# One of eight encoder blocks: which weight tiles are summed by transfers, by ones and by VectorE

## The chip, the core and the metric

The kernel runs on one core of one Trainium2 chip. The metric is the device time of one execution in microseconds (us), median of several executions. TensorE (PE) multiplies matrices, VectorE (DVE) works on whole tiles elementwise, ScalarE (ACT) computes functions such as tanh and exp, GpSimd (POOL) here mostly issues transfers, and SyncE (SP) only issues transfers. Sixteen DMA engines move the data.

## The reference, cut to what matters

Two graph attention layers stand behind one another, each added to its input; N is 4096 nodes, with four heads of 128 features. The change lies in the encoder, the first attention of the first layer:

```python
h = jnp.maximum(_layernorm(x, axis=-1), 0.0)
Xw = jnp.einsum('hnd,hde->hne', Xh, W)            # per head
f1 = jnp.einsum('hnd,hd->hn', Xw, V[:, 0, :, 0])
f2 = jnp.einsum('hnd,hd->hn', Xw, V[:, 1, :, 0])
sig = jax.nn.sigmoid(f1[:, :, None] + f2[:, None, :])
att = _masked_softmax(adj[None] * sig, adj != 0)   # local and long pattern are both adj
Xa = jnp.einsum('hij,hjd->hid', att, Xw)
Xn = _batchnorm(Xc, enc_bn_gamma, enc_bn_beta)     # Xc: the heads side by side
```

So each output row is a sum over neighbours of weight times value, divided by the sum of the same weights. That second sum, the denominator, is what the change concerns. After the encoder come a matrix product with batch normalization, a decoder that uses the same weights again, another product, and the second layer with an attention of its own.

## The kernel before

**Tiles and blocks.** Weights are made transposed: a tile `e` holds 128 source nodes (partitions) by 2048 target nodes. An attention works through blocks; a block is one head `h` and one half `tb` of the targets, so there are eight, numbered n = 0 to 7. "Block three" below is n = 2, the first half of head two; "block four" is n = 3. In a block, `j` runs over 32 source tiles. The whole encoder is one loop over n and j in `attention` (lines 395 to 516).

**What happens for one j.** A buffer is taken for `e` (line 420). ScalarE computes a tanh into it (line 570) and an exp in place (line 571). VectorE multiplies it with the adjacency tile `a` (line 572). TensorE multiplies it with the head's values in four matrix products, one for each 512 targets, which accumulate over j in four PSUM banks `po` (line 469). The third and fourth step of the same loop make the sum for the denominator, in one of three ways, chosen by j:

- *moved* (line 489): GpSimd issues two accumulating transfers, one for each half of the tile, that add `e` to a second sum tile named `acc` in the profile (`into` in the code). The first moved tile of a block is copied instead, which overwrites the old sum.
- *by ones* (line 267): TensorE multiplies the tile with a 128 by 32 matrix of ones, four narrow products next to each other in the array, into the bank `den`. Neighbouring j of this kind are held back and done together.
- *added* (lines 497 and 499): VectorE adds the tile to `acc`. The first such instruction takes two tiles.

At j = 31 both sum tiles are themselves multiplied with ones into `den` (lines 514 and 516). The next block's first moved tile has to wait for that, because it overwrites the sum tile that this product reads.

**Buffers.** `weight_tile` (line 254) deals out eight buffers in turn: two shared with the decoder and six of the block (`ebufs` is 6, plus `EP` = 2). As 32 is a multiple of eight, tile j always gets the buffer of tile j − 8, and ScalarE's tanh into it waits until everyone who reads tile j − 8 is done: its matrix products, its sum (transfers included), and for every fifth tile (j = 4, 9, 14, ...) a store to memory that the decoder reads later.

**The end of a block, inside the next.** VectorE copies the four banks out in step j = 2 of the next block (line 682), copies `den` at j = 4 (line 273), and inverts the row sums at j = 10 (lines 283 and 284). GpSimd's queue, which is in order, carries the hops of the row sums between its moves: `dens` out and `dcol` in at j = 4, `rinvs` at j = 10, four loads of `rb` from j = 11 on (lines 274, 279, 287, 292). A move behind such a hop waits for it. VectorE scales and takes statistics as these arrive (lines 686 and 689).

**Choice by block.** `modes` (line 401) gives each block its moved and its by-ones tiles:

```python
ENC_FIRST = (), (5, 6, 11, 12, 17, 18, 24, 25, 30, 31)
ENC_SECOND = (12, 14, 17, 19, 22, 24, 26), (1, 2, 4, 5, 7, 8, 30, 31)
ENC = (0, 2, 5, 7, 10, 12, 15, 17, 20, 22, 25), (8, 9, 30, 31)
```

`ENC` holds for n = 2 to 7. The core of the sums:

```python
if j in moved:
    for into_half, e_half in in_parts(2, into, e):
        nc.gpsimd.dma_start(into_half, e_half, **({"accum_op": ALU.add} if j > moved[0] else {}))
elif j in by_ones:
    held.append(e)
```

In block three SyncE also loads the 1 MB of encoder weights (`encoder_weights`, at j = 8).

Of the kernel before, what the change touches and what calls it, by code (L numbers as in the profile page):

```python
# [60 lines left out]

ENC_FIRST = (), (5, 6, 11, 12, 17, 18, 24, 25, 30, 31)
ENC_SECOND = (12, 14, 17, 19, 22, 24, 26), (1, 2, 4, 5, 7, 8, 30, 31)
ENC = (0, 2, 5, 7, 10, 12, 15, 17, 20, 22, 25), (8, 9, 30, 31)

GAT_FIRST = (0, 2, 4, 6, 8, 10, 12, 14, 16, 18, 20, 22, 24), (30, 31)
# [23 lines left out]
def kernel(ctx, tc, x, xT, adjT, w0, w0T, v0, wencT, wdecT, vecs, w1, w1T, a1, outT):  # L90
# [486 lines left out]
    with tc.tile_pool(name="keep", bufs=1) as keep:  # L577

        with tc.tile_pool(name="f_small", bufs=1) as small, tc.tile_pool(name="f_work", bufs=2) as work:
# [5 lines left out]
            for ib in range(NIB):  # L585
# [7 lines left out]
                for c in range(0, C, 1 if ib == 0 else C):  # L593
                    n = 1 if ib == 0 else C
# [125 lines left out]
        with tc.tile_pool(name="enc", bufs=1) as spool:  # L720

            with tc.issue_after(last_copy.ins), tc.issue_after(masks0[-1][1].ins):
                attention("enc", keep, spool, tanh_weights, R[0:4], lambda h, tb: (rows[tb], h), out_enc,
                          (scaled, statistics), 6, lambda n: (ENC_FIRST, ENC_SECOND, ENC)[min(n, 2)],
                          (TINY, ALU.max), "write", row0=row0, masks0=masks0,
                          extras={(2, 8): encoder_weights, (H * NTB - 1, 10): coefs_of_three,
                                  (H * NTB - 1, 12): bias_of_three, (H * NTB - 1, 20): scale_three})
# [399 lines left out]
```

## Time and profile before

| | us |
|---|---|
| median of three executions | 3204.63 (3203.29 to 3204.93) |
| the profiled execution | 3203.78 |
| span from its first to its last instruction | 3202.0 |

| engine | busy us | share of the span |
|---|---|---|
| TensorE | 3144.9 | 98% |
| VectorE | 2937.1 | 92% |
| ScalarE | 2573.6 | 80% |
| GpSimd | 526.1 | 16% |

The mean granted TensorE clock is 0.997. The encoder takes roughly the first 1034 us of the span. Times below are us from the span's start; a block is counted from the end of the last matrix product of the block before it to the end of its own last one: block two ends at 320.4, block three at 438.9, block four at 559.1, then every 118.2 up to 913.7. In the list of groups an entry gives line, engine, operation, tiles, count, total busy time, mean duration and the idle time ahead of it. In a timeline an entry gives start, duration, engine, line, operation, number of merged instructions, and in brackets the idle time ahead of it with what ended it. A start to the next start is a little shorter than the duration, as neighbouring instructions of an engine overlap by about 0.1 us.

### The profile page before, as it was taken

The page shows a single profiled execution, that of the slowest core. Times are in us where ns is not written, and L with a number is a line of the kernel's source. Part 1 is how long each engine was busy: PE and PEld are TensorE (multiplying, and loading weights), DVE is VectorE, ACT ScalarE, POOL GpSimd, SP SyncE. Part 2 cuts the span into 40 slices and gives each one's busy share as a digit, 9 for nine tenths or more (in the row PEclk, how much of TensorE's full clock was granted, in tenths as well). Part 3 has the DMA queues.
Part 4 walks back from the last instruction along what each step waited for, and adds up shares of the span by engine and source line. Part 5 has one row for each costly group of instructions (what it writes and reads, how often), then busy time and mean ns, then how long its engine had stood idle before and what let it go on. Part 6 is the DMA issues. An engine that isn't in the chain of part 4 may idle for free.

```text
span 3202.0 us, 30044 instructions
## 1 busy us (share of the span) xinstructions
PE 3144.9 (98%) x10531; PEld 1369.0 (43%) x10531; DVE 2937.1 (92%) x2221; ACT 2573.6 (80%) x1825; POOL 526.1 (16%) x684
## 2 busy tenths in 40 slices
PE   7999999999999999999999999999999999999998
PEld 6334444444444463333333333458544444444443
DVE  7989999999999679999999999785699999999998
ACT  7999999999998449999999999466755665666663
POOL 3001211211211000010100100026312222222211
PEclk9999999999999999999999999999999999999999
DMA  9999988988987014445445454231579999999996
GB/s 211 198 194 253 269 225 229 268 220 230 273 232 194 7 41 147 158 144 169 156 161 166 144 170 145 91 110 63 155 189 233 215 222 241 218 214 230 236 213 156
DMA packets 215367, 591.33 MB, mean 185 GB/s; under 512 B 25936, under 2 KB 29040, under 8 KB 199216
## 3 DMA queue, kind: packets, MB, share of 16 engines
q0 software_dynamic: 71584, 234.05, 38.3%
q1 hardware_dynamic: 132200, 332.53, 30.2%
q10 hardware_dynamic: 11432, 22.85, 2.0%
q8 instruction: 82, 1.34, 0.2%
q14 instruction: 69, 0.57, 0.1%
HBM read 378.15 MB, written 84.30 MB: 144 GB/s over the span
## 4 chain that ended last, share of the span: by engine, by line
PE 55%; DVE 22%; issue 10%; DMA 9%; ACT 4%; DVEq 0%; POOL 0%; ACTq 0%; SPq 0%; POOLq 0%
PE ps L331 22%; PE ps L469 14%; PE ps L738 7%; DVE e L1044 7%; DVE R L499 6%; DMA w<-e 6%; DVE e L572 4%; PE den L331 3%; PE ps L949 3%; DVE acc L499 3%; DMA a<-mask 3%; ACT e L570 2%; PE den L267 2%; ACT e L571 1%; PE ps L798 1%
## 5 line engine op out<-in xcount | busy, mean ns | idle before, releaser
L469 PE MATMUL ps<-e,R 128*128 128x512 f32 x3992 | 1738.0, 595 | 25.9 <-DVE e L572 21.5
L469 PEld LDWEIGHTS ps<-e,R 128*128 128x128 f32 x3992 | 753.4, 190 | 1006.8 <-issue 919.6
L572 DVE TENSOR_TENSOR e<-e,a 128x2048 f32<-128x2048 f32 (+1 forms) x470 | 1050.0, 2262 | 88.2 <-ACT e L571 75.3
L570 ACT ACTIVATE e<-rowb,score 128x2048 f32<-128x2048 f32 (+1 forms) x470 | 909.5, 1970 | 25.0 <-PE ps L331 9.0
L571 ACT ACTIVATE e<-e 128x2048 f32<-128x2048 f32 (+1 forms) x470 | 866.9, 1880 | 6.4 <-DVE e L572 3.0
L331 PE MATMUL ps<-e,R 128*64 128x512 f32 x2624 | 746.9, 592 | 1.6 <-DVE e L572 1.5
L1043 ACT ACTIVATE e<-rowb,nq,jcol 128x2048 f32<-128x2048 f32 x224 | 459.6, 2088 | 263.2 <-DMA w<-e 133.8
L1044 DVE SCALAR_TENSOR_TENSOR e<-e,jcol,a 128x2048 f32<-128x2048 f32 (+1 forms) x265 | 592.0, 2266 | 2.8 <-ACT e L1043 2.8
L331 PEld LDWEIGHTS ps<-e,R 128*64 128x64 f32 x2624 | 241.8, 137 | 319.8 <-issue 316.2
L499 DVE TENSOR_TENSOR R<-R,e 128x2048 f32<-128x2048 f32 x128 | 291.7, 2279 | 0.0
L499 DVE TENSOR_TENSOR acc<-acc,e 128x2048 f32<-128x2048 f32 x121 | 276.4, 2284 | 0.9
L489 POOL DMA_DIRECT2D w<-e x178 | 149.2, 847 | 610.7 <-DMA w<-e 282.4
L738 PE MATMUL ps<-R,w 128*128 128x512 f32 x512 | 220.4, 592 | 0.6 <-DVE w L696 0.6
L489 POOL DMA_DIRECT2D acc<-e x146 | 122.6, 891 | 520.9 <-DMA acc<-e 212.6
L331 PE MATMUL den<-e,R 128*64 128x512 f32 x320 | 149.8, 592 | 0.0
L738 PEld LDWEIGHTS ps<-R,w 128*128 128x128 f32 x512 | 97.1, 190 | 123.0 <-issue 117.4
L331 PE MATMUL ps<-e,w 128*64 128x512 f32 x288 | 138.1, 592 | 0.7 <-DVE e L572 0.7
L292 POOL DMA_DIRECT2D rb<-rinvs x60 | 33.8, 568 | 521.0 <-DVE R L686 453.3
L949 PE MATMUL ps<-w1x,hT 128*128 128x260 f32 x512 | 115.5, 384 | 1.4 <-ACT hT L927 1.4
L331 PE MATMUL ps<-t,w 128*64 128x512 f32 x336 | 111.2, 592 | 1.0 <-DVE t L340 1.0
L949 PEld LDWEIGHTS ps<-w1x,hT 128*128 128x128 f32 x512 | 96.5, 190 | 19.9 <-issue 3.3
L331 PE MATMUL ps<-t,R 128*64 128x512 f32 x192 | 90.2, 592 | 0.0
(209 smaller groups left out, 2109.9 us busy)
## 6 DMA issues: line engine op xcount, KB each, us to landing
a<-mask SPq DMA_DIRECT2D x720, 256.0 KB, 4.2
w<-e POOLq DMA_DIRECT2D x178, 512.0 KB, 6.7
acc<-e POOLq DMA_DIRECT2D x146, 512.0 KB, 6.9
e<-ekeep SPq DMA_DIRECT2D x48, 1024.0 KB, 5.1
ekeep<-e SPq DMA_DIRECT2D x36, 1024.0 KB, 6.9
mask<-in_adjT POOLq DMA_DIRECT2D x8, 2048.0 KB, 105.3
rowb<-rows SPq DMA_DIRECT2D x16, 1024.0 KB, 6.1
rb<-rinvs POOLq DMA_DIRECT2D x60, 256.0 KB, 4.8
```

Source lines behind the costliest of these rows:

```text
L267: last_ones = nc.tensor.matmul(den[s * 32:(s + 1) * 32, :], ones[:, 0:32], t[:, s * IB:(s + 1) * IB], start=start, stop=stop)
L331: last_half = nc.tensor.matmul(b[g * HD:(g + 1) * HD, :], weight, x, start=start, stop=stop)
L469: last_main = nc.tensor.matmul(b, block(values[h], j), e[:, s * IB:(s + 1) * IB], start=(j == 0), stop=(j == NJ - 1))
L489: nc.gpsimd.dma_start(into_half, e_half, **({"accum_op": ALU.add} if j > moved[0] else {}))
L499: nc.vector.tensor_add(acc, acc, e)
L570: nc.scalar.activation(e, rowb, AF.Tanh, bias=column(score[:, 1], j, h), scale=0.5)
L571: last_act = nc.scalar.activation(e, e, AF.Exp, scale=0.5)
L572: last_dve = nc.vector.tensor_mul(e, e, a)
L738: last = nc.tensor.matmul(z, w[:, fb, o * P:(o + 1) * P], nodes(src[fb], ib), start=(fb == 0), stop=(fb == C - 1))
L949: m = nc.tensor.matmul(banks[k][:, 0:2 * DX], hT[:, fb, c * P:(c + 1) * P], w1x[:, fb, 2 * k:2 * k + 2, :].rearrange("p h x -> p (h x)"), ...
L1043: last_act = nc.scalar.activation(e, rowb, AF.Relu, bias=column(nq, j, h), scale=column(jcol, j, h))
L1044: last_dve = nc.vector.scalar_tensor_tensor(e, e, column(jcol2, j, h), a, ALU.add, ALU.mult)
```

## The change

Block three (n = 2) gets a choice of its own; all other blocks keep theirs.

```diff
 ENC_SECOND = (12, 14, 17, 19, 22, 24, 26), (1, 2, 4, 5, 7, 8, 30, 31)
+ENC_THIRD = (0, 3, 6, 9, 12, 15, 18, 21, 24), (7, 8, 16, 30, 31)
 ENC = (0, 2, 5, 7, 10, 12, 15, 17, 20, 22, 25), (8, 9, 30, 31)
...
-                          (scaled, statistics), 6, lambda n: (ENC_FIRST, ENC_SECOND, ENC)[min(n, 2)],
+                          (scaled, statistics), 6, lambda n: (ENC_FIRST, ENC_SECOND, ENC_THIRD, ENC)[min(n, 3)],
```

In block three nine tiles are moved instead of eleven, each three steps after the last instead of two and three in turn. Five tiles instead of four are summed by ones (7, 8, 16, 30, 31 for 8, 9, 30, 31). The remaining eighteen instead of seventeen are added by VectorE, in seventeen instructions instead of sixteen.

## The prediction

> **What bounds the kernel now.** The page puts TensorE at 98% of the span, but a change to one block must be read in that block. So I first cut the encoder by blocks in the table of windows, then asked who waits for whom in block three, then read the timelines of ScalarE, GpSimd, TensorE and VectorE there. The windows of blocks two to five (length; busy time of PE, PEld, DVE, ACT, POOL; clock; DMA share):
>
> ```profile
> 206.00:320.40 114.40, 111.06 (x295) 46.41 (x297) 108.35 (x60) 111.04 (x60) 15.54 (x21) 1.00 0.95 236
> 320.40:438.90 118.50, 116.59 (x309) 49.52 (x312) 113.32 (x63) 112.42 (x61) 22.37 (x29) 1.00 0.90 247
> 438.90:559.10 120.20, 118.13 (x308) 50.11 (x310) 114.47 (x64) 120.20 (x66) 22.38 (x29) 0.99 0.88 237
> 559.10:677.30 118.20, 116.57 (x309) 49.51 (x312) 114.36 (x64) 118.20 (x65) 22.35 (x29) 1.00 0.90 241
> ```
>
> From block four on ScalarE is busy for the whole window: 120.20 of 120.20, 118.20 of 118.20. One tile costs it 3.693 us (two tanh and two exp start every 7.386 us), so 32 tiles cost 118.2 us, the length of a block. The list of waits of ScalarE between 404 and 1030 us is empty. From block four to the end of the encoder ScalarE sets the pace, and whatever delays it earlier is carried along to the end. Block three is the last in which it waits, 6.1 us (118.50 − 112.42). Who makes it wait there (total, times, longest):
>
> ```profile
> POOL acc L489 <- DMA acc<-e: 36.5, 12, 6.0
> ...
> DVE e L572 <- ACT e L571: 5.0, 5, 2.3
> ACT e L570 <- DMA acc<-e: 4.4, 3, 2.5
> ...
> ACT e L570 <- issue: 0.6, 1, 0.6
> ```
>
> The timeline of ScalarE shows where:
>
> ```profile
> 360.14 2.00 ACT L570 ACTIVATE e<-rowb,score 128x2048 f32<-128x2048 f32 x1 [1.63 <-DMA acc<-e]
> ...
> 390.75 2.00 ACT L570 ACTIVATE e<-rowb,score 128x2048 f32<-128x2048 f32 x1 [0.61 <-issue]
> ...
> 400.78 2.00 ACT L570 ACTIVATE e<-rowb,score 128x2048 f32<-128x2048 f32 x1 [2.54 <-DMA acc<-e]
> ```
>
> Counting two tiles per pair from the block's start, these are the tanh of tiles 15, 23 and 25; a fourth wait, 0.23 us before tile 20 at 380.75, is not shown. Their buffers were those of 7, 15, 17 and 12: all four are moved tiles, none is a stored one. GpSimd's timeline confirms it, the "issue" one too, since the next move into the same half of the sum waits for the same landing:
>
> ```profile
> 381.17 0.86 POOL L489 DMA_DIRECT2D acc<-e  x1 [2.27 <-DMA acc<-e]
> ...
> 390.96 0.85 POOL L489 DMA_DIRECT2D acc<-e  x1 [2.12 <-DMA acc<-e]
> ...
> 400.96 0.86 POOL L489 DMA_DIRECT2D acc<-e  x1 [2.26 <-DMA acc<-e]
> ```
>
> These are the second halves of tiles 15, 17 and 20: each issues 0.2 to 0.4 us after ScalarE was released (at 380.75, 390.75, 400.78). With that of tile 12 at 371.58 they come 9.6, 9.8 and 10.0 us apart. Eleven moves ask for one every 2.5 steps, 9.2 us. The chain of transfers is slower than its timetable, falls behind, and ScalarE runs into it.
>
> [...] TensorE is busiest on the page, but the gaps that travel are ScalarE's. [...] a median of 6.9 us for accumulating halves over the encoder, and up to 10 us in block three with the DMA engines at a 0.90 share; I use the trace's. [...] eight of them, two tiles by ones, take 1.85 us.
>
> **The change part by part.**
>
> *Transfers.* Two tiles less: four issues of about 0.86 us on GpSimd and 2 MB less to move. Spacing is now three steps, 11.1 us, against the 9.6 to 10.0 a move takes. I walk through the queue, since its hops come between. Tile 0 as before at 323.4, when the old sum has been read. Tile 3 takes the place of tile 2 at 327.3 and 329.5. The `dcol` hop holds the queue until 341.2 as before; behind it tile 6 (in place of 5) at 341.8, then tile 9 (in place of 7) at 347.4 and 350.7, landed by 359.9. The `rb` loads end at 362.3; then tile 12, landed about 368.7 and 371.6, which is when the halves of tile 10 let the next ones go before. Tile 15 then issues at these times and lands near 381; 18 near 390; 21 near 400; 24 near 412. A dense ScalarE wants the buffer of 9 (for tile 17) at 365, of 12 (for 20) at 378, of 15 (for 23) at 388, of 18 (for 26) at 401, of 21 (for 29) at 410 and of 24 (for tile 0 of block four) at 423. All land earlier, by 5 to 11 us. Tile 7, which stalled ScalarE first, goes by ones: TensorE finishes tile 8 near 355.1 and the ones at 356.9, and tile 15 wants the buffer at 358.5.
>
> *What ScalarE gains.* Its pair (12, 13) starts at 349.14. Without a wait tanh 25 would start at 349.14 + 6 × 7.386 + 1.89 = 395.35; it started at 400.78. The gain is 5.43 us: the four waits (5.01) and the overlap lost at each.
>
> *VectorE, one add more, 2.20 us.* Its idle time between 354 and 405 us is five waits for ScalarE, 5.03 us in all, which go with the stalls. From 322 us I add up the new order: until tile 9 it does as many adds as before (1, 2, 4, 5 for 1, 3, 4, 6); tiles 10 and 11 both need one, so it reaches tile 12 1.4 us later than before, 356.3 for 354.85; tile 14 at 362.9, tile 16 at 369.5 as soon as it is made, tile 20 at 385.1, tile 22 at 391.7 as soon as it is made. From there 10 multiplies and 7 adds of 2.20 and four short ones of 0.60 come to 39.8, so tile 31 is masked at 431.5 instead of 435.1. So VectorE pays its 2.2 out of waits that vanish and still comes 3.6 earlier.
>
> *TensorE, one tile by ones more.* About 0.95 us: half of 1.85, and a switch of its own since tile 16 stands alone. TensorE's line:
>
> ```profile
> 360.29 51.77 PE L469 MATMUL ps<-e,R 128*128 128x512 f32 x120
> 412.56 17.50 PE L469 MATMUL ps<-e,R 128*128 128x512 f32 x40 [0.50 <-DVE e L572]
> 430.77 3.70 PE L469 MATMUL ps<-e,R 128*128 128x512 f32 x8 [0.70 <-DVE e L572]
> 435.18 3.70 PE L469 MATMUL ps<-e,R 128*128 128x512 f32 x8 [0.70 <-DVE e L572]
> ```
>
> It is dense until 412.06 and idles 1.9 us after that for VectorE, which is now earlier. So block three ends near 438.9 − 1.9 + 0.95 = 437.9, one microsecond earlier, bound by TensorE. The rest of ScalarE's gain is not lost but not yet cashed: the waits of TensorE in the next blocks (120.20 − 118.13 = 2.07 in block four, 1.63 each in blocks five to seven) are all for VectorE, which had waited for ScalarE. They hold 1.0 + 2.1 + 3 × 1.63 = 8.0 us, more than 5.43. VectorE, delayed at the copies of line 682 until TensorE ends block three (1.8 us earlier than before), has 5.6 us of waits for ScalarE in block four to catch up with. So the ends of blocks move by about −1, −3, −4.8 and then the full −5.4.
>
> *What could be late next.* In block four the same chain runs with eleven moves: its tiles 12, 15 and 17 landed at 497.6, 507.4 and 514.5, and ScalarE wanted the buffers at 502.4, 511.7 and 519.1, a slack of 4.3 to 4.8. ScalarE comes 5.4 earlier; the chain comes about 3 earlier, because it starts from the row sums that VectorE inverts at 468.1, now near 465. That leaves about 2 us of slack. Where it is not enough, up to 1.1 us (5.43 − 4.3) comes back as a wait. Stores of every fifth tile land 9 us ahead of need and don't bind.
>
> *Sum.* 3202.0 − 5.4 = 3196.6 of span, 3198.4 with the 1.78 around it. Block eight is bound by TensorE from its start (120.21 busy of 120.30) and all behind the encoder follows from its end, so I carry the shift through at full value. The profiled execution lies 0.85 below the median of the runs shown; from the median the forecast is 3204.63 − 5.4 = 3199.2, a fall of 0.17%. A measurement of this kernel can tell about 0.2%, 6.4 us, from no change, so this counts as within it.
>
> **Rivals.**
>
> - *Part of the stalls returns.* In block four, as worked out, or because a transfer in block three takes longer than its slot. For it: the slack of 2 us. Against: less traffic, later slots. Half the gain: 3204.6 − 2.7 = 3201.9.
> - *VectorE takes over.* One mechanism for slower: if VectorE's 5.0 us of waits don't go with the stalls (the schedule puts adds ahead of multiplies that TensorE needs late in the block), its 2.2 us delay the last masked tile, then TensorE and ScalarE's buffers: 3204.6 + 2.2 = 3206.8. It decides once less than 2.2 of those 5.0 us can be filled. Against it: VectorE had 5.6 us more in block four.
> - *More than ScalarE's own waits.* The order of the queues or the dips of the clock (0.87 between 532 and 545 us) fall otherwise; another 1.6 us, block four's extra TensorE time, would go: 3197.6.
>
> **How the numbers follow.** The forecast has a chance of 0.57, part returning 0.23, VectorE 0.10, more 0.10. The range: its low end, 3197.0, takes in most of the third rival; its high end, 3203.6, all of the part that returns up to a gain of 1 us. Outside are the slower case and the edges, about 0.18. Faster by over 0.2%, below 3198.2: nearly all of "more" and the lower edge of the forecast's own spread of 1 us, 0.20. Slower by over 0.2% needs 6.4 us, three times what VectorE's add can cost: 0.03. The rest, 0.77, lies within.
>
> **What would show it.** Right: ScalarE without a wait for `acc<-e` after 322 us; tanh 25 near 395.4; block ends near 437.9, 556, 672.5, then 118.2 apart; GpSimd idle between moves for VectorE rather than for transfers. Wrong: a wait of ScalarE for `acc<-e` in block four, a VectorE without idle time up to the end of block four, or a last masked tile after 435.1.

## The result, and the profile after

The changed kernel takes 3198.74 us (median of 18 executions), the kernel before 3204.07 (median of 18 on the same chip): a ratio of 0.9982 with a 95% interval of 0.9975 to 0.999, 5.3 us less. The profiled execution has a span of 3197.1 us against 3202.0.

The windows of blocks three, four and five of the changed kernel (columns as before: length, busy time of PE, PEld, DVE, ACT and POOL, clock, DMA share, GB/s):

```profile
320.40:437.30 116.90, 116.90 (x316) 49.92 (x315) 116.73 (x66) 115.82 (x64) 19.02 (x25) 1.00 0.84 234
437.30:553.80 116.50, 116.06 (x309) 49.84 (x312) 112.91 (x62) 116.50 (x64) 22.45 (x29) 1.00 0.89 242
553.80:671.90 118.10, 116.47 (x308) 49.41 (x305) 114.25 (x64) 118.10 (x65) 22.29 (x29) 1.00 0.89 240
```

Block three is 1.6 us shorter than before, block four 3.7, block five 0.1. So most of what the change in block three saves shows up one block later. In block three TensorE is now busy for all of the 116.90 us, and VectorE for 116.73.

ScalarE's waits from 322 to 1030 us, all of them, in the list of waits (time, times, longest), and from its timeline the tanh of tiles 24 and 25:

```profile
ACT e L571 <- PE den L268: 1.1, 1, 1.1
```

```profile
393.52 3.88 ACT L571 ACTIVATE e<-rowb,score 128x2048 f32<-128x2048 f32 x2
```

The one wait left lies before tile 5 at 321.5 and was there before the change. The tanh of tile 25 is the second of the pair and starts at 393.52 + 1.89 = 395.41, where it had started at 400.78.

The two halves of tile 18, of 21, and of 24 (merged) in GpSimd's timeline:

```profile
380.80 0.85 POOL L490 DMA_DIRECT2D acc<-e  x1 [5.20 <-DVE e L573]
386.74 0.85 POOL L490 DMA_DIRECT2D acc<-e  x1 [5.09 <-DMA acc<-e]
390.87 0.85 POOL L490 DMA_DIRECT2D acc<-e  x1 [3.28 <-DVE e L573]
396.23 0.86 POOL L490 DMA_DIRECT2D acc<-e  x1 [4.51 <-DMA acc<-e]
404.14 1.75 POOL L490 DMA_DIRECT2D acc<-e  x2 [7.05 <-DVE e L573]
```

GpSimd now waits for VectorE to finish the tile at the first half of each, and at tile 24 neither half waits for a landing. The chain of transfers keeps up with its timetable. Before, both halves of tiles 15, 17, 20 and 22 waited for a landing.

TensorE's timeline at the ends of blocks three and four:

```profile
385.59 51.77 PE L470 MATMUL ps<-e,R 128*128 128x512 f32 x120
437.28 1.92 PE L268 MATMUL den<-e,ones 128*32 128x512 f32 x16
...
477.24 72.37 PE L470 MATMUL ps<-e,R 128*128 128x512 f32 x168
550.05 3.70 PE L470 MATMUL ps<-e,R 128*128 128x512 f32 x8 [0.44 <-DVE e L573]
```

The three waits for VectorE at the end of block three are gone, and so is the one in block four, of which 0.44 is left. Before the change it stood here:

```profile
532.82 26.31 PE L469 MATMUL ps<-e,R 128*128 128x512 f32 x56 [1.90 <-DVE e L572]
```

The clean measure is the length from the start of the last sums by ones of block two to the start of the first of the four leftover products at the encoder's end (line 532 before, 533 after), because blocks one and two differ by up to 3.0 us from execution to execution. It was 1034.18 − 322.08 = 712.10 us and is 1028.79 − 322.14 = 706.65: a gain of 5.45. The kernel before was profiled once. From there to the end of the span it takes 2167.8 us before and 2168.3 after, both within the 2166.2 to 2168.3 seen over these two and the ten runs below.

### The profile page after: what moved, and what is told of

Read it like the earlier page. It is cut to its first block, busy times and chain, and to the rows that moved or that the text cites. A ratio compares the mean times of both kernels' runs of the same rounds, so it can differ in the third digit from the quotient of the medians.

```text
span 3197.1 us, 30054 instructions
## 1 busy us (share of the span) xinstructions
PE 3146.9 (98%) x10539; PEld 1371.7 (43%) x10539; DVE 2938.7 (92%) x2222; ACT 2573.7 (81%) x1825; POOL 525.9 (16%) x680
## 4 chain that ended last, share of the span: by engine, by line
PE 68%; DVE 15%; issue 8%; ACT 5%; DMA 3%; DVEq 0%; ACTq 0%; POOL 0%; POOLq 0%; SPq 0%
PE ps L470 28%; PE ps L332 22%; PE ps L739 7%; DVE e L573 5%; DVE acc L500 4%; PE den L332 3%; PE ps L950 3%; ACT e L571 3%; DMA a<-mask 3%; DVE R L500 2%; ACT e L572 2%; DVE e L1045 2%; PE den L268 1%; PE ps L799 1%; PE ps L658 1%
```

## The experiments

**Places or number of moves.** The changed numbers (nine moved, five by ones, eighteen added), the moves at the old places:

```diff
-ENC_THIRD = (0, 3, 6, 9, 12, 15, 18, 21, 24), (7, 8, 16, 30, 31)
+ENC_THIRD = (0, 2, 5, 7, 10, 12, 15, 17, 20), (8, 9, 16, 30, 31)
```

> Block three with nine moves, five tiles by ones and eighteen added, as in the changed kernel, but the moves at the old places (0, 2, 5, 7, 10, 12, 15, 17, 20), and by ones 8, 9, 16, 30, 31. Theory A (ScalarE's waits for the buffers of moved tiles are the whole effect, and the spacing decides): the transfers up to tile 20 run as before, so the waits before tiles 15, 20, 23 and 25 stay, tanh 25 starts near 400.8 us, and the time is that of before, within 1 us. Theory B (two transfers and 2 MB less are the effect): about 5 us faster, as the changed kernel.

3203.11 us, ratio 1.0 (0.9991 to 1.0008); length 711.75, a gain of 0.35. ScalarE's timeline:

```profile
360.05 2.01 ACT L571 ACTIVATE e<-rowb,score 128x2048 f32<-128x2048 f32 x1 [1.54 <-DMA acc<-e]
...
390.47 2.00 ACT L571 ACTIVATE e<-rowb,score 128x2048 f32<-128x2048 f32 x1 [0.75 <-issue]
...
400.44 2.00 ACT L571 ACTIVATE e<-rowb,score 128x2048 f32<-128x2048 f32 x1 [2.47 <-DMA acc<-e]
```

The same waits at the same tiles, with 2 MB less to move. Only the 0.23 us before tile 20 has gone. The smaller number pays nothing without the wider spacing. This run also shows that the extra add and the extra sum by ones are covered even with the waits in place.

**Ten moves, three apart, with VectorE's adds as before.**

```diff
-ENC_THIRD = (0, 3, 6, 9, 12, 15, 18, 21, 24), (7, 8, 16, 30, 31)
+ENC_THIRD = (0, 3, 6, 9, 12, 15, 18, 21, 24, 27), (7, 8, 16, 30, 31)
```

> Block three with ten moves three steps apart (0, 3, ..., 27), by ones 7, 8, 16, 30, 31, so VectorE adds seventeen tiles as before. Theory A: ScalarE doesn't wait in block three, tanh 25 near 395.4 us, encoder 5.4 us earlier as in the changed kernel, since VectorE's extra add cost nothing there. Theory B (number of transfers): about half, 2.7 us faster. If VectorE's add does cost: faster than the changed kernel by up to 2.2 us.

3199.86 us, ratio 0.9988 (0.998 to 0.9996); length 708.21, a gain of 3.89. ScalarE doesn't wait in block three, as theory A said; tanh 25 starts at 393.78 + 1.89 = 395.67, in an execution that began the block 0.3 later. So the spacing decides there, not the number of moves. But a wait came back in block four, before its tile 25:

```profile
515.40 2.00 ACT L571 ACTIVATE e<-rowb,score 128x2048 f32<-128x2048 f32 x1 [1.45 <-DMA acc<-e]
```

It and the overlap lost at it make up the missing 1.56. This is the rival "part of the stalls returns", at the place it named. Block four's choice is the same as in the changed kernel; there the second half of its tile 17 landed just before 512.75, when the next move went out behind it, and ScalarE took the buffer at 513.6. Here it landed 2.8 us later. The slack is about one microsecond. The chain lags from the block's second move on (445.56 us for 444.26) and at the hop (454.39 for 452.67); what holds it up there is open.

**Block four instead of block three.**

```diff
-(ENC_FIRST, ENC_SECOND, ENC_THIRD, ENC)[min(n, 3)]
+(ENC_FIRST, ENC_SECOND, ENC, ENC_THIRD, ENC)[min(n, 4)]
```

> The new choice in block four (n = 3) instead of block three, which keeps the old one. Theory A: ScalarE has no waits in block four to lose and keeps those of block three, so the end of the encoder stays within 0.5 us of before. Theory B (the mix with fewer transfers is cheaper in itself): about 5 us faster. If TensorE's 0.95 or VectorE's 2.2 us were uncovered: 1 to 2 us slower.

3203.54 us, ratio 1.0 (0.9992 to 1.0009); length 712.27, 0.17 longer. The new mix is worth nothing in itself: it pays where ScalarE waited, and only there.

**Three more adds on VectorE.**

```diff
-ENC_THIRD = (0, 3, 6, 9, 12, 15, 18, 21, 24), (7, 8, 16, 30, 31)
+ENC_THIRD = (0, 3, 6, 9, 12, 15, 18, 21, 24), (30, 31)
```

> The changed kernel with only tiles 30 and 31 by ones in block three; VectorE adds 7, 8 and 16 too, three more, 6.6 us, and TensorE saves three sums by ones, 2.8 us. Theory A: VectorE is dense in block three already, so its last masked tile comes 6.6 us later than in the changed kernel, near 438.6; the chain of transfers in block four starts some 2 us later than before the change while ScalarE is 5.4 earlier, so ScalarE waits there about 3.4 us; some 2 us of the gain remain (3202 us). Rival C (every add on VectorE is paid in full): 1.2 us slower than before. Rival D (VectorE's cover is still not used up): 5.4 us faster.

3202.51 us, ratio 0.9995 (0.9987 to 1.0003), which alone tells little; length 710.16, a gain of 1.94, of which the expectation said 2. In block three ScalarE doesn't wait. Its waits come in blocks four and five:

```profile
506.52 2.00 ACT L571 ACTIVATE e<-rowb,score 128x2048 f32<-128x2048 f32 x1 [0.33 <-DMA acc<-e]
...
516.39 2.00 ACT L571 ACTIVATE e<-rowb,score 128x2048 f32<-128x2048 f32 x1 [2.37 <-DMA acc<-e]
...
635.18 2.00 ACT L571 ACTIVATE e<-rowb,score 128x2048 f32<-128x2048 f32 x1 [0.50 <-DMA acc<-e]
```

Their sum is 3.20 (3.4 was expected). VectorE's last tile of block three was masked at 438.4 instead of 432.1, and the first move of block four went out at 445.1 instead of 440.4. So the cover for VectorE ends between one add and four. Past it the price was here not the adds' own time but the later start of the next block's transfers, on which ScalarE then waited.

**Why block three.** The kernel before, with the load of the encoder weights moved to a later step of block three:

```diff
-extras={(2, 8): encoder_weights, ...
+extras={(2, 27): encoder_weights, ...
```

> The kernel before with one change: SyncE's 1 MB load of the encoder weights in block three moved from j = 8 to j = 27, behind the last moves; all sums as before. Question: why block three alone falls behind with the choice that holds in block four. Theory A1 (the load shares the DMA engines with the first moves and the row sums' hop, which took 10.3 us of waiting on GpSimd in block three and 6.0 in block four): the hop is 4 to 5 us shorter, ScalarE's waits before tiles 15, 20, 23 and 25 shrink to under 1 us, and the encoder ends 4 to 5 us earlier, with eleven moves. Theory A2 (eleven moves are too many there, load or not): waits as before, no change.

3199.72 us, ratio 0.9988 (0.9981 to 0.9994); length 707.87, a gain of 4.23 with all eleven moves kept. The row sums' hop in GpSimd's timeline, which took 10.27 us of waiting in the kernel before, and the one wait for a transfer that ScalarE has left:

```profile
336.91 0.58 POOL L279 DMA_DIRECT2D dcol<-dens  x1 [5.72 <-DMA dens<-dsb]
```

```profile
396.96 2.00 ACT L570 ACTIVATE e<-rowb,score 128x2048 f32<-128x2048 f32 x1 [1.10 <-DMA acc<-e]
```

Theory A1 holds, but for one wait of 1.10 us where under 1 was expected. In the kernel before, SyncE issues the 1 MB at 324.8 us, among the first moves. Without it the wait for the hop, 8 KB, is 4.6 us shorter, and what stands behind the hop in GpSimd's queue goes out sooner: tile 12 at 355.9 instead of 362.3. Whether the 1.10 us at 396.96 come from the late load is open. With this one wait, the choice with eleven moves was fit for a block without that load at its start.

**The new choice everywhere.** In all blocks from three on:

```diff
-(ENC_FIRST, ENC_SECOND, ENC_THIRD, ENC)[min(n, 3)]
+(ENC_FIRST, ENC_SECOND, ENC_THIRD)[min(n, 2)]
```

> The new choice in all blocks from three to eight (n = 2 to 7). Theory A: after block three ScalarE had no waits left to lose, and VectorE's 2.2 us a block fit into its 3.5 to 3.7 us of waits for ScalarE, TensorE's 0.95 into its 1.6: the end of the encoder as in the changed kernel, within 0.5 us, that is 5.4 us before the kernel before. Rival (cheaper mix pays in each block): another 5 us a block. Rival (VectorE is full): up to 2 us a block slower, 11 us.

3197.60 us, ratio 0.998 (0.9973 to 0.9986), not to be told from the changed kernel's; length 707.73, that is 1.08 longer than the changed kernel, where 0.5 was allowed. That is a miss, and it lies in block eight, as the run with all blocks but that one shows below.

**And the stores of block two on SyncE.** As the last, and:

```diff
-if stores and (store if n > 1 else j % KEEP == KEEP - 3):
+if stores and (store if n > 0 else j % KEEP == KEEP - 3):
...
-(nc.sync if n > 1 else nc.scalar).dma_start(ekeep[h][tb][k], t)
+(nc.sync if n > 0 else nc.scalar).dma_start(ekeep[h][tb][k], t)
```

> As the run with the new choice in all blocks, and besides in block two the stores for the decoder are issued by SyncE, as from block three on, not by ScalarE. In block two ScalarE's own queue stands 3.0 us behind stores that wait for VectorE, and 1.1 us for the last one's buffer at the start of block three. Theory A (ScalarE's waits before it turns dense count one for one, now that transfers have room in all blocks): the encoder ends 2 to 4 us earlier than with the changed kernel, near 1025 to 1027 us. Rival (TensorE or VectorE bind in blocks two and three): the same as the changed kernel, as TensorE has no wait left in block three.

3197.99 us, ratio 0.9985 (0.9979 to 0.9992); length 706.06, end of the encoder at 1028.82. A miss: 2 to 4 us were expected. ScalarE's own queue no longer stands behind stores in block two, but it waits there 3.5 us for a store's landing and 2.4 for moves instead. One wait was exchanged for others. The shorter length is not the stores' doing: to the end of block seven it is that of the run before (586.26 us for 586.34). Block eight makes the difference, through TensorE's pace, as shown below.

**Both remedies.** The changed kernel with the late load.

> The changed kernel with SyncE's load of the encoder weights at j = 27 of block three, both remedies together. Theory A (both take away the same waits of ScalarE): nothing to add, the encoder ends as in the changed kernel, near 1028.8 us, within 0.5. Rival (the two gains are of different kinds): 4 us further, near 1025.

3198.17 us, ratio 0.9982 (0.9973 to 0.999); length 706.65, the changed kernel's to the hundredth. The two take away the same waits.

**All but block eight.**

```diff
-(ENC_FIRST, ENC_SECOND, ENC_THIRD, ENC)[min(n, 3)]
+(ENC_FIRST, ENC_SECOND, *[ENC_THIRD] * 5, ENC)[n]
```

> The new choice in blocks three to seven, the old one in block eight. The run with it in all blocks ended the encoder 1.3 us later than the changed kernel. Theory A: that is TensorE's extra sum by ones, 0.95 us, in block eight, where TensorE has no wait; without it the encoder ends within 0.5 us of the changed kernel, near 1028.8. Rival (VectorE falls behind block by block): 1030 as before.

3197.68 us, ratio 0.9981 (0.9974 to 0.9988); length 706.65. So the 1.08 us of the run in all blocks come with the choice in block eight, and in blocks three to seven an extra add and an extra sum by ones per block cost nothing.

But that TensorE has no wait in block eight, as the expectation says, holds only in some executions. In seven of the twelve profiled executions, this one and the one with all blocks among them, TensorE has no wait there but is slower. In two of the seven, of the kernel before and of the changed kernel, its mean granted clock was 0.89 between 957 and 973 us, and 152 products in a row took 67.53 us. In one of the other five, with ten moves, the mean clock of block eight was 1.00 and 104 products took 44.88 us: 0.43 each, as in block three (51.77 for 120). From TensorE's pace I take it that the clock dipped in all seven and in none of the five; for the other nine that is an estimate. In the four of the five with the old choice in block eight TensorE waits for VectorE instead, as in the changed kernel's second execution (next run):

```profile
1006.86 20.87 PE L470 MATMUL ps<-e,R 128*128 128x512 f32 x48 [1.78 <-DVE e L573]
```

The new choice in block eight ran once with the dip (all blocks) and once without (all blocks, stores on SyncE). The same 40 instructions in both, ahead of the extra sum by ones:

```profile
958.22 19.11 PE L470 MATMUL ps<-e,R 128*128 128x512 f32 x40
...
958.54 17.41 PE L470 MATMUL ps<-e,R 128*128 128x512 f32 x40
```

From the end of block seven to the leftover products it took 121.39 us with the dip and 119.80 without, against 120.55 in both executions of the changed kernel, one with the dip and one without. So TensorE has about 1.8 us to spare in block eight, the 1.78 of the wait above. The dip uses them up, and only then does the extra sum by ones, 1.00 us long, make the block longer. This rests on one execution of each kind.

**The changed kernel again.**

> The changed kernel once more on the same chip as the two others: encoder's end at 1028.8 within 0.5 us if it is set by ScalarE's dense stretch; ratio to before near 0.998.

3197.88 us, ratio 0.9982 (0.9973 to 0.999). The encoder's end came at 1031.23, 2.4 later than expected, because in that execution block three began 2.4 later; the length is 706.65 again. My expectation should have named the length, not the time of day.

| | length, us | gain | ratio to before |
|---|---|---|---|
| before | 712.10 | | |
| changed | 706.65 | 5.45 | 0.9982 |
| nine moves, old places | 711.75 | 0.35 | 1.0 |
| ten moves, three apart | 708.21 | 3.89 | 0.9988 |
| block four alone | 712.27 | −0.17 | 1.0 |
| three more adds | 710.16 | 1.94 | 0.9995 |
| before, late load | 707.87 | 4.23 | 0.9988 |
| all blocks | 707.73 | 4.37 | 0.998 |
| all blocks, stores on SyncE | 706.06 | 6.04 | 0.9985 |
| changed, late load | 706.65 | 5.45 | 0.9982 |
| blocks three to seven | 706.65 | 5.45 | 0.9981 |
| changed, again | 706.65 | 5.45 | 0.9982 |

No version is measurably faster than the changed kernel. The 0.59 us between 706.65 and 706.06 are block eight's, in the one execution with the new choice there and no dip; why VectorE no longer holds TensorE up there is open. For blocks three to seven, once ScalarE runs without a wait from tile 5 of block three on (busy for 116.50 of 116.50 us in block four and 118.10 of 118.10 in block five), only a faster ScalarE or an earlier start is left.

## Why the prediction was right

- *ScalarE sets the pace and its waits travel to the end.* Shown. A gain of 5.43 us was worked out from its timeline; the encoder shortened by 5.45. In the runs with waits left, the gain is the 5.45 less what ScalarE waits after tile 5 of block three, and less some 0.1 us of overlap for each wait: with the late load 1.10, leaving 4.23; with ten moves 1.45, leaving 3.89; with three more adds 3.20 in three waits, leaving 1.94. Only the two runs with the new choice in block eight depart from this.
- *The waits are for moved tiles, and spacing ends them.* Shown by the runs with nine moves at the old places (waits stay) and ten at the new ones (none in block three).
- *The walk through GpSimd's queue.* The `dcol` hop came at 341.7 for 341.2 and tile 12 at 363.4 for 362.3. From there its landings were mis-sized: the second half of tile 15 landed near 386.5, when that of 18 could go out, for 381, and that of 18 near 396 for 390, since these halves took 9 to 12 us each. Of the 5 to 11 us of room that I gave, tile 15 had 1.5 left (tanh 23 starts at 386.14 + 1.89 = 388.03). The sign held because three steps, 11.1 us, are long enough for each half to land before its buffer is wanted, not by the margin that I worked out, 7 us for this tile; that so little was enough was partly luck. That VectorE's tiles would be what first halves wait for was right from tile 18 on. Earlier first halves, and the second halves up to tile 21, went on waiting for landings or hops.
- *VectorE's extra add is covered.* An add took 2.28 us, 2.20 from start to start. VectorE masked the last tile at 432.1, for 431.5; the sum of its work held to 0.6 us. The rival in which VectorE takes over did not come. The run with three more adds shows where it would: between 2.2 and 8.8 us.
- *TensorE's extra sum by ones.* 1.00 us (384.59 to 385.59 in its timeline) for 0.95. The timeline gives its eight narrow products 1.06 us, and eight of the wide ones 3.70. Block three ended at 437.3 for 437.9; the end of block four at 553.8 for 556. The second difference is a term that I had taken over as fixed: block four's TensorE time of 118.13 us held a dip of the clock, 0.89 between 530 and 545 us, which did not occur in the changed execution (1.00 there). It shortened the road to the full gain by a block and changed nothing of its size.
- *Slack in block four.* About 2 us were said; the changed execution had about 1. That is the weakest term of the working. The ten-move run shows that such a wait does come back.
- *Carried through to the end.* In the profiled execution 4.9 of the 5.4 us arrive at the end of the span; the rest is within the scatter of what follows the encoder. In the medians all of it arrives, 5.3. The reason that I gave for block eight was wrong, though. I took it as bound by TensorE, busy for 120.21 of 120.30 us, but the execution that I read had the dip of the clock there (0.89 between 957 and 973 us). The block takes 120.55 us with the dip and without it, and without it TensorE waits 1.78 us for VectorE, which in turn waits five times for ScalarE in this block (5.2 us in the first execution of the changed kernel). So the shift came through, but not because TensorE sets the end.

What I had not seen is why block three alone fell behind: I took the slow chain as given, with the load in plain sight. Moving that load alone brings 4.23 of the 5.45 us.

## What to carry to other kernels

Look for the last wait of the engine that is dense (busy without a gap) from there on. Here ScalarE's waits in block three, 5.01 us and the overlap lost at each, were worth 5.45 at the end of the encoder, though GpSimd stood 36.5 us waiting for transfers in that block and only 1.6 of the gain was seen before the next. Before changing a balance that holds in five of six blocks, look for what the sixth has besides; here one load at the wrong moment cost nearly as much as the new balance won. A cover must be counted block by block, and in more than one execution: an extra sum by ones that was free in five blocks came with 1.08 us in block eight, in an execution where a dip of the clock had used up TensorE's spare time there (19.11 us for products that took 17.41 in another).

## What the runs showed that I had not expected

- A hop of 8 KB through memory cost GpSimd a wait of 9.3 to 10.7 us in five profiled executions with the 1 MB load beside it (before, changed, nine moves, and the two with the new choice in all blocks), 5.7 in the two without, in the same place of the same block.
- A busy share close to 100% hid spare time. In the changed kernel's first execution TensorE was busy for 120.41 of block eight's 120.50 us, with a mean granted clock of 0.89 over 16 us; in its second it waited 1.78 us there, and the length of the block was 120.55 us in both.
- The stretch from block three to the encoder's end repeats to 0.01 us (706.65 in four profiled executions: the changed kernel twice, with the late load, and with the new choice in blocks three to seven), while blocks one and two moved its start by up to 3 us. By my estimate from this a length from mark to mark tells 0.2 us apart, where the intervals of the ratios, 0.0006 to 0.0009 to either side, stand for 2 to 3 us.
